# Two of four tiles turned by VectorE and moved in SBUF, in a two-layer kernel on one TensorE

## The chip, the cores and the metric

The kernel runs on one core of one Trainium2 chip. The metric is the device time of one execution in microseconds (us). A core has TensorE (PE in the profile; its weight loads are PEld), VectorE (DVE), ScalarE (ACT), GpSimd (POOL) and SyncE (SP), which issues most of the DMAs. SBUF is the working memory; TensorE writes to PSUM, which has eight banks of 128 x 512 fp32 here.

## The reference

Two transformer layers with a layer norm behind each part, on x of 2 x 512 x 512. Only what the change stands between is shown: the linear attention of layer 0, and behind its norm the quantized feed-forward part.

```python
# layer 0, linear attention (one query head in four is used)
q_sel = (elu(x @ Wq.T + bq) + 1)[:, :, ::G, :]
num = einsum('bshd,hde->bshe', q_sel, M)
den = einsum('bshd,hd->bsh', q_sel, z)[..., None] + EPS
x = layernorm(x + repeat(num / den, G, axis=2).reshape(b, s, H * D) @ Wo.T)
# layer 0, quantized feed-forward; weights are -s, 0 or s
xf = x / 128.0
inter = silu(xf @ w_gate.T) * (xf @ w_up.T)
inter_q = trunc(clip(inter * 128, -128, 127))
x = layernorm(x + trunc(clip(inter_q @ w_down.T * 128, -128, 127)))
# layer 1: softmax attention with one head, then a SwiGLU part, each with a layer norm
```

## The kernel before

x is held as eight tiles of 128 rows x 512, four for each of the two sequences (`xs[b][t]`; `order` lists them as tiles 0 to 7, `NT` is 4). Layer 0's attention first computes the queries, then folds the memory M with the output weights into `mw`.

The stage around the change is the loop over `order` (L677). For each tile, `read` (L550) makes eight products of 128x128 by 128x512 (L561), one per head, each into a PSUM bank of its own; an fp32 product shows as two instructions. The last column of each product is the denominator: ScalarE copies it out (L565), VectorE takes the reciprocal of four at a time (L569). Of the eight heads three are scaled by ScalarE (L574) and added by GpSimd (L578, L590), five are added to x by VectorE (L583). The norm of the tile before (`norm_a0`, L660: statistics on VectorE, the root on GpSimd, the shift at L668 on VectorE and the application at L669 on ScalarE) is put between.

Behind the loop stands the quantized layer, `up` (L733): for each of eleven chunks of the inner width and each sequence, two times eight products in fp32r (L741) with the transposed rows as the moving operand. fp32r keeps fewer bits than fp32, so the rows go in as a high part (a copy rounded to fp32r) and a low part (the rest): `split` (L262) makes both, four column blocks each.

The two sequences get their transposed rows in different ways:

- The first sequence: within tiles 5, 6 and 7 (`halfway`, and behind the tile), TensorE transposes one column block of all four tiles (L275, four transposes into one bank), ScalarE copies it to the high part (L280) and VectorE subtracts for the low part (L281). The high parts lie in one tile of the pool `xtp` (two slots), the low parts in two of the pool `wop` (four slots).
- The second sequence: VectorE turns each tile in squares of 32 x 32 (`turn_squares`, L675), and `move_squares` (L286) moves the squares to their places with 16 SBUF-to-SBUF DMAs over SP, GpSimd and ScalarE (L296). `split(1, xt1)` then copies and subtracts from SBUF.

The first sequence's rows are needed when the loop ends; the second's when six chunks of the first are done (`LEAD`). The down weights' loads wait on SP behind the move.

What sets the order: GpSimd's instructions are issued as written. For the other engines a list scheduler orders them at build time, by the order of the program among those that its cost model holds for ready, so an instruction written later can be issued earlier on its engine. `tc.issue_after(ins)` ties what is written under it to be issued behind `ins`, but only instructions of the same engine as `ins`. On the chip every engine goes through its list in order, and a waiting instruction holds all behind it.

Of the kernel before, what the change touches and what calls it, by code (L numbers as in the profile page):

```python
# [19 lines left out]
P = 128  # L20
# [19 lines left out]
def kernel(  # L40
# [221 lines left out]
    def split(b, xt=None):  # L262


        hi = xtp.tile([P, NK, S], F32, tag="xt", name=f"xh_{b}").bitcast(F32R)
        los = [pair_tile(f"xl_{b}_{i}").bitcast(F32R) for i in range(2)]
        his = [hi[:, k, :] for k in range(NK)]
        los = [los[k // 2][:, k % 2, :] for k in range(NK)]

        def block(k):  # L270
            h, l = his[k], los[k]
            if xt is None:
                rows = psum(f"pt_f0{b}_{k}")
                for t in range(NT):
                    nc.tensor.transpose(rows[:, ts(t, P)], xs[b][t][:, ts(k, P)], ident)  # L275
            else:
                rows = xt[:, :, k, :]
                h, l = (u.rearrange("p (t q) -> p t q", t=NT) for u in (h, l))
            return (
                nc.scalar.copy(h, rows),  # L280
                nc.vector.tensor_sub(l, rows, h.bitcast(F32)),  # L281
            )
# [3 lines left out]
    def move_squares(squares, xt, three=True):  # L286
# [4 lines left out]
        for i in range(P // SQ):  # L291
            for j in range(P // SQ):
                eng = nc.gpsimd if i == j else nc.sync
                if i == (j + 2) % 4:
                    eng = nc.gpsimd if not three else nc.scalar if i else nc.sync
# [8 lines left out]
    def pair_tile(name):  # L304
        return wop.tile([P, 2, HID], F32, tag="wo", name=name)
# [75 lines left out]
    with tc.tile_pool(name="a0w", bufs=1) as a0w, tc.tile_pool(name="a0", bufs=2) as a0:  # L381
# [168 lines left out]
        def read(b, t, halfway, between):  # L550
# [3 lines left out]
            for h0 in range(0, NH, 4):  # L554
                if h0:
                    halfway()
# [114 lines left out]
        x2 = []  # L671

        def turn_squares(i):
# [3 lines left out]
        for i, (b, t) in enumerate(order):  # L677
            steps = read(
                b, t, lambda: block(2 * (i - NT) - 3) if i > NT + 1 else None,
                lambda steps: norm_a0(i - 1, steps) if i else None,  # L680
            )
# [6 lines left out]
            if i == 5:  # L688
                parts, block = split(0)
                x2.append(parts)  # L690
                squares = xtp.tile([P, NT, HID], F32, tag="xt", name="squares")
            if i in (5, 6):
                block(2 * (i - NT) - 2)
            if i > NT:
                turn_squares(i - 1)
        norm_a0(len(order) - 1, steps)
        turn_squares(len(order) - 1)
# [858 lines left out]
```

## Time and profile before

| | us |
|---|---|
| median of three runs (lowest, highest) | 457.17 (457.02, 457.43) |
| the profiled execution | 458.13 |
| its span, first to last instruction | 456.4 |
| TensorE busy | 448.6 |
| VectorE busy | 309.8 |
| ScalarE busy | 259.6 |
| GpSimd busy | 113.7 |

The granted TensorE clock was 0.996 of full speed over the span. In the profile a line such as `106.95 0.44 PE pt_f L275 x4` of the chain in order of time is a start, a length, the engine, the tile written, the line of the program and a count. In the groups of instructions the numbers behind the first bar are the busy time in us and the mean of one in ns; behind the second bar stands the engine's idle time before them, and who ended it. In the timeline the bracket gives the idle time before an instruction and who ended it. Matmul records in the profile overlap, since they are pipelined; their starts tell the pace.

### The profile page before, as it was taken

The numbers are of one execution on the slowest core, as the hardware profiler recorded it, in microseconds if no ns is written. First come the engines' busy times: TensorE is split into PE (matmuls) and PEld (weight loads), VectorE is DVE, ScalarE is ACT, GpSimd is POOL, SyncE is SP. The second block draws the span as 40 slices with busy tenths as digits, with TensorE's granted clock in tenths as the row PEclk, the third lists the DMA queues.
The fourth block names the chain that finished last, engine by engine and source line by source line (L and its number), as shares of the span: only waits on it lengthen the run. The fifth ranks groups of instructions, "written<-read, shape, count | busy, mean of one in ns | idle before, by whom it ended". The sixth has DMA issues, their size and how long they took to land.

```text
span 456.4 us, 5785 instructions
## 1 busy us (share of the span) xinstructions
PE 448.6 (98%) x1913; PEld 337.0 (74%) x1913; DVE 309.8 (68%) x617; ACT 259.6 (57%) x492; POOL 113.7 (25%) x160
## 2 busy tenths in 40 slices
PE   8999999999999999999999999999999999999995
PEld 8887753344588888888766578888888888888884
DVE  3976658777867788856978799545534547777524
ACT  4887986466657974557746645454545446433311
POOL 0200304575640059200372336100000000011211
PEclk9999999999999999999999999999999999999998
DMA  8999981000027201121495601300000000000001
GB/s 278 376 281 314 180 294 46 0 3 0 2 44 198 103 3 48 47 93 37 152 371 87 101 0 31 63 0 1 0 0 1 0 2 0 1 15 33 37 34 69
DMA packets 33172, 38.18 MB, mean 84 GB/s; under 512 B 20656, under 2 KB 21552, under 8 KB 33136
## 3 DMA queue, kind: packets, MB, share of 16 engines
q1 hardware_dynamic: 27440, 30.65, 20.3%
q0 software_dynamic: 2240, 6.29, 7.5%
q10 hardware_dynamic: 3456, 0.75, 0.8%
q8 instruction: 22, 0.36, 0.3%
q14 instruction: 14, 0.11, 0.1%
HBM read 32.45 MB, written 2.10 MB: 76 GB/s over the span
## 4 chain that ended last, share of the span: by engine, by line
PE 92%; DMA 2%; ACT 2%; DVE 1%; issue 1%; SPq 0%; POOL 0%; POOLq 0%
PE pu L1248 23%; PE pd L1248 12%; PE po L561 10%; PE pq L504 9%; PE pg_f L741 9%; PE pu_f L741 9%; PE pd_f L800 4%; PE pqk L1061 3%; PE pu L1293 2%; PE pv L1078 2%; PE pot L1123 2%; PE psc L1017 2%; PE po L1140 2%; DMA gu<-in_gu 1%; DMA wq<-in_wq 1%; PE pmw L545 1%
## 5 line engine op out<-in xcount | busy, mean ns | idle before, releaser
L561 PE MATMUL po<-mw,q 128*128 128x512 f32 x128 | 57.3, 598 | 0.7 <-ACT y L574 0.5
L1248 PE MATMUL pu<-r,ugu 128*128 128x512 f32 x200 | 48.6, 389 | 0.0
L146 POOL TENSOR_TENSOR rstd_f<-mv_f,ln_eps 128x1 f32<-128x1 f32 x15 | 6.1, 409 | 168.7 <-DVE mv_f L1416 128.0
L339 ACT ACTIVATE pu<-pu 128x512 f32<-128x512 f32 x42 | 24.1, 580 | 41.2 <-PE pu L1248 37.4
L561 PEld LDWEIGHTS po<-mw,q 128*128 128x128 f32 x128 | 22.9, 189 | 31.4 <-issue 18.5
L1248 PEld LDWEIGHTS pu<-r,ugu 128*128 128x128 f32 x200 | 37.5, 188 | 7.8
L170 ACT ACTIVATE ta_f<-y_f,below_half 128x512 int8<-128x512 f32 (+1 forms) x22 | 15.9, 721 | 27.4 <-DVE y_f L158 27.1
L583 DVE SCALAR_TENSOR_TENSOR x<-po,den,x 128x511 f32<-128x511 f32 x40 | 29.8, 745 | 1.8
L578 POOL TENSOR_TENSOR y<-y,y 128x511 f32<-128x511 f32 x16 | 21.1, 1319 | 24.9 <-DVE x L583 20.8
L1248 PE MATMUL pu<-r,it_early 128*128 128x512 f32 x104 | 24.9, 389 | 0.0
L767 DVE SCALAR_TENSOR_TENSOR it_f<-tb_f,ta_f 128x512 fp32r<-128x512 int16 (+1 forms) x22 | 15.2, 690 | 13.8 <-ACT tb_f L171 13.8
L741 PE MATMUL pg_f<-xh,tu 128*128 128x512 f32 x88 | 24.4, 399 | 0.0
L1307 DVE TENSOR_TENSOR it_f<-ev,pu 128x512 f32<-128x512 f32 x20 | 13.6, 683 | 15.5 <-PE pu L1248 14.9
L1136 ACT ACTIVATE x<-x,off_f,rstd_f 128x512 f32<-128x512 f32 x7 | 5.7, 816 | 32.0 <-POOL off_f L1135 32.0
L741 PE MATMUL pg_f<-xl,tu 128*128 128x512 f32 x88 | 23.6, 390 | 0.0
L741 PE MATMUL pu_f<-xh,tu 128*128 128x512 f32 x88 | 23.5, 389 | 0.0
L741 PE MATMUL pu_f<-xl,tu 128*128 128x512 f32 x88 | 23.5, 389 | 0.0
L1248 PE MATMUL pd<-ugu,r 128*128 128x512 f32 (+1 forms) x79 | 22.5, 362 | 0.0
L1248 PEld LDWEIGHTS pu<-r,it_early 128*128 128x128 f32 x104 | 19.5, 188 | 4.0
L351 POOL TENSOR_SCALAR td<-wd,inv_down 128x512 fp32r<-128x512 f32 x11 | 20.1, 1846 | 1.6 <-DVE inv_down L206 1.6
L800 PE MATMUL pd_f<-td,it_f 128*128 128x512 f32 x88 | 20.3, 389 | 0.0
L565 ACT ACTIVATE den<-po,den_eps 128x1 f32<-128x1 f32 x64 | 13.6, 271 | 11.1 <-PE po L561 11.0
(382 smaller groups left out, 1089.6 us busy)
## 6 DMA issues: line engine op xcount, KB each, us to landing
gu<-in_gu SPq DMA_DIRECT2D x20, 512.0 KB, 7.4
wd<-in_wd SPq DMA_DIRECT2D x20, 256.0 KB, 4.7
wo<-in_wo SPq DMA_DIRECT2D x8, 512.0 KB, 9.7
wo<-in_wo POOLq DMA_DIRECT2D x8, 512.0 KB, 9.1
wq<-in_wq SPq DMA_DIRECT2D x8, 256.0 KB, 4.9
x<-in_x SPq DMA_DIRECT2D x7, 256.0 KB, 5.1
out<-x SPq DMA_DIRECT2D x7, 256.0 KB, 2.0
x<-in_bo POOLq DMA_DIRECT2D x4, 256.0 KB, 6.1
```

Of the source, the lines that this page charges most:

```text
L170: nc.scalar.activation(a[:n], y, AF.Relu, bias=below_half[:n])
L339: return nc.scalar.activation(p, p, AF.Copy, scale=BIG + 1.0)
L351: eng.tensor_scalar(out, w, factor, None, ALU.mult)
L504: done = nc.tensor.matmul(p, w, x, start=(start and i == 0), stop=(i == len(todo) - 1), skip_group_check=not start,)
L561: nc.tensor.matmul(po, qs[b][h0 + j][:, ts(t, P)], mw[:, h0 + j, :], start=True, stop=True,)
L578: nc.gpsimd.tensor_add(ys[0][:, :LAST], ys[0][:, :LAST], y[:, :LAST])
L583: steps.append(nc.vector.scalar_tensor_tensor(x[:, :LAST], four[j][:, :LAST], d, x[:, :LAST], ALU.mult, ALU.add))
L741: nc.tensor.matmul(pp[a], t[:, a, i % NK, :], x2[b][i], start=(i == 0), stop=(i == 2 * NK - 1),)
L767: nc.vector.scalar_tensor_tensor(it[:n], tb[:n], 128.0, ta[:n], ALU.min, ALU.subtract)
L800: nc.tensor.matmul(pd, inter[b][c][:, ts(t, P)], td[c].bitcast(F32R), start=(c == 0), stop=(c == last),)
L1061: nc.tensor.matmul(p, wqkv[:, k, ts(j, D)], xt[:, k, :], start=(k == 0), stop=(k == NK - 1),)
L1248: done = nc.tensor.matmul(p, w, x, start=(start and i == 0), stop=(i == n - 1), skip_group_check=not start,)
```

## The change

Of the first sequence, tiles 0 and 1 are now turned in squares by VectorE (in the iterations 1 and 2) and moved by 16 DMAs, all issued by SP, with half the bytes each; tiles 2 and 3 are transposed by TensorE tile by tile, four column blocks of one tile into one bank, in iterations 4 and 5. The copies and subtractions go by tile in place of by column block: two halves of 128 x 256 for each tile, from PSUM for tiles 2 and 3 and from the moved squares for tiles 0 and 1 (iterations 5 and 6). The subtractions (and whatever else is VectorE's) of the latter are tied behind the first L583 of their tile. `read` loses its `halfway`. The high and low parts of the first sequence now lie in four tiles of `wop`, those of the second in the two slots of `xtp`. For the other moves nothing is changed.

```diff
+    def split_squares(b, xt):
+        hi, lo = (
+            xtp.tile([P, NK, S], F32R, tag="xt", name=f"x{part}_{b}") for part in "hl"
+        )
+        his, los = units(hi), units(lo)
         def block(k):
-            h, l = his[k], los[k]
-            if xt is None:
-                rows = psum(f"pt_f0{b}_{k}")
-                for t in range(NT):
-                    nc.tensor.transpose(rows[:, ts(t, P)], xs[b][t][:, ts(k, P)], ident)
-            else:
-                rows = xt[:, :, k, :]
-                h, l = (u.rearrange("p (t q) -> p t q", t=NT) for u in (h, l))
+            h, l = (u[k].rearrange("p (t q) -> p t q", t=NT) for u in (his, los))
+            rows = xt[:, :, k, :]
             return (
                 nc.scalar.copy(h, rows),
                 nc.vector.tensor_sub(l, rows, h.bitcast(F32)),
...
+    def split_tiles(b):
+        pairs = [pair_tile(f"x_{b}_{i}", F32R) for i in range(NK)]
+        def part(t, rows):
+            done = []
+            for i in range(2):
+                h, l = (pairs[j + i][:, :, ts(t, P)] for j in (0, 2))
+                src = rows[:, 2 * i : 2 * i + 2]
+                done += [nc.scalar.copy(h, src), nc.vector.tensor_sub(l, src, h.bitcast(F32))]
+            return done
+        def turned(t):
+            rows = psum(f"pt_f0{b}_{t}")
+            for k in range(NK):
+                nc.tensor.transpose(rows[:, ts(k, P)], xs[b][t][:, ts(k, P)], ident)
+            return rows.rearrange("p (k q) -> p k q", k=NK)
+        return [u for p in pairs for u in units(p)], part, turned
...
-    def move_squares(squares, xt, three=True):
+    def move_squares(squares, xt, queues=3):
...
-                eng = nc.gpsimd if i == j else nc.sync
+                eng = nc.gpsimd if i == j and queues > 1 else nc.sync
-                if i == (j + 2) % 4:
-                    eng = nc.gpsimd if not three else nc.scalar if i else nc.sync
+                if i == (j + 2) % 4 and queues > 1:
+                    eng = nc.gpsimd if queues == 2 else nc.scalar if i else nc.sync
...
+        TURNED = NT // 2
         for i, (b, t) in enumerate(order):
-            steps = read(
-                b, t, lambda: block(2 * (i - NT) - 3) if i > NT + 1 else None,
-                lambda steps: norm_a0(i - 1, steps) if i else None,
-            )
+            steps = read(b, t, lambda steps: norm_a0(i - 1, steps) if i else None)
...
-            if i == 5:
-                parts, block = split(0)
+            if i == 1:
+                squares0 = xtp.tile([P, NT, HID], F32, tag="xt", name="squares_0")
+                xt0 = xtp.tile([P, NT, NK, P], F32, tag="xt", name="xt_f00")
+            if 1 <= i <= TURNED:
+                turn_squares(i - 1, squares0)
+            if i == TURNED:
+                move_squares(squares0[:, :TURNED], xt0[:, :TURNED], queues=1)
+            if i == NT:
+                parts, part, turned = split_tiles(0)
                 x2.append(parts)
+                part(TURNED, turned(TURNED))
+            elif i == NT + 1:
                 squares = xtp.tile([P, NT, HID], F32, tag="xt", name="squares")
-            if i in (5, 6):
-                block(2 * (i - NT) - 2)
+                part(NT - 1, turned(NT - 1))
+            if NT + 1 <= i <= NT + TURNED:
+                with tc.issue_after(steps[0].ins):
+                    part(i - NT - 1, xt0[:, i - NT - 1])
             if i > NT:
-                turn_squares(i - 1)
+                turn_squares(i - 1, squares)
...
-        parts, block = split(1, xt1)
+        parts, block = split_squares(1, xt1)
```

More of the change, by code (lines that the diff above doesn't have):

```diff
@@ L260, in down_weights @@
         return wds
[L262 to L268, printed above, removed]
-        def block(k):
-            h, l = his[k], los[k]
-            if xt is None:
-                rows = psum(f"pt_f0{b}_{k}")
-                for t in range(NT):
-                    nc.tensor.transpose(rows[:, ts(t, P)], xs[b][t][:, ts(k, P)], ident)
-            else:
-                rows = xt[:, :, k, :]
-                h, l = (u.rearrange("p (t q) -> p t q", t=NT) for u in (h, l))
+    def split_squares(b, xt):
[3 more added lines that the diff above has]
+        his, los = units(hi), units(lo)
+        def block(k):
+            h, l = (u[k].rearrange("p (t q) -> p t q", t=NT) for u in (his, los))
+            rows = xt[:, :, k, :]
             return (
@@ L302, with pair_tile @@
     wop = ctx.enter_context(tc.tile_pool(name="wop", bufs=4))
-    def pair_tile(name):
-        return wop.tile([P, 2, HID], F32, tag="wo", name=name)
+    def pair_tile(name, dtype=F32):
+        return wop.tile([P, 2, HID], dtype, tag="wo", name=name)
     def spare_tile(name, dtype=F32):
@@ L548, in fold, with read @@
             nc.scalar.activation(mw[:, h, :LAST], p[:, :LAST], AF.Identity, bias=c)
-        def read(b, t, halfway, between):
+        def read(b, t, between):
             x = xs[b][t]
@@ L554, in read @@
             for h0 in range(0, NH, 4):
-                if h0:
-                    halfway()
                 four = []
@@ L671, with turn_squares @@
         x2 = []
-        def turn_squares(i):
+        TURNED = NT // 2
+        def turn_squares(i, squares):
             b, t = order[i]
@@ L687 @@
                 flag_up, eff_up = verdict(tot_up, sc_up, "up")
-            if i == 5:
-                parts, block = split(0)
+            if i == 1:
[7 more added lines that the diff above has]
+                parts, part, turned = split_tiles(0)
                 x2.append(parts)
+                part(TURNED, turned(TURNED))
+            elif i == NT + 1:
                 squares = xtp.tile([P, NT, HID], F32, tag="xt", name="squares")
-            if i in (5, 6):
-                block(2 * (i - NT) - 2)
+                part(NT - 1, turned(NT - 1))
+            if NT + 1 <= i <= NT + TURNED:
+                with tc.issue_after(steps[0].ins):
+                    part(i - NT - 1, xt0[:, i - NT - 1])
             if i > NT:
-                turn_squares(i - 1)
+                turn_squares(i - 1, squares)
         norm_a0(len(order) - 1, steps)
-        turn_squares(len(order) - 1)
+        turn_squares(len(order) - 1, squares)
     fp = ctx.enter_context(tc.tile_pool(name="fp", bufs=2))
@@ L1225 @@
     xt_r1 = fp.tile([P, NT, NK, P], F32, tag="it10", name="xt_f11", bufs=1)
-    move_squares(squares, xt_r1, three=False)
+    move_squares(squares, xt_r1, queues=2)
     def rows_from_squares(k):
```

## The prediction

> **What bounds the kernel now.** I read the page first: the engines' shares and the chain that ended last. TensorE is busy nearly all the time, and 92% of the chain is TensorE.
>
> ```profile
> span 456.4 us, 5785 instructions
> ...
> PE 448.6 (98%) x1913; PEld 337.0 (74%) x1913; DVE 309.8 (68%) x617; ACT 259.6 (57%) x492; POOL 113.7 (25%) x160
> ```
>
> Next the chain in order of time, in the stage that the diff touches: the reading of the memory (L561), with four groups of four transposes (L275) between its products. Right behind it stands the first product of the quantized layer (L741).
>
> ```profile
> 99.98 6.97 PE po L561 x16
> 106.95 0.44 PE pt_f L275 x4
> 107.39 3.44 PE po L561 x8
> 110.82 0.52 PE pt_f L275 x4
> 111.35 3.65 PE po L561 x8
> 114.99 0.44 PE pt_f L275 x4
> 115.43 3.44 PE po L561 x8
> 118.86 0.44 PE pt_f L275 x4
> 119.30 3.44 PE po L561 x8
> 122.74 1.84 PE pg_f L741 x8
> ```
>
> So the sixteen transposes of the first sequence lie on the path, 0.44+0.52+0.44+0.44 = 1.84 us of it. From 122.74 to 445.5 us the chain is TensorE without a stall worth naming, so what TensorE gains here should reach the end, unless another engine hands over late.
>
> Which other engine is close? The eight products of tile 2 take 6.87 us of TensorE, undisturbed (first products start at 78.44 and 85.31). In the chain, 6.97 against 6.87, 0.52 against 0.44 and 3.65 against 3.44 are waits of 0.10, 0.08 and 0.21 us, 0.39 together, for a PSUM bank: there are eight, a tile has eight products, and VectorE (L583) or ScalarE (L574) frees each. These two form a loop, and the timeline of VectorE shows it:
>
> ```profile
> 84.15 0.17 DVE L569 RECIPROCAL den<-den 128x4 f32<-128x4 f32 x1
> 84.41 0.75 DVE L583 SCALAR_TENSOR_TENSOR x<-po,den,x 128x511 f32<-128x511 f32 x1
> 87.45 0.18 DVE L569 RECIPROCAL den<-den 128x4 f32<-128x4 f32 x1 [2.29 <-ACT den L565]
> ...
> 91.48 0.17 DVE L569 RECIPROCAL den<-den 128x4 f32<-128x4 f32 x1
> ```
>
> From the first reciprocal of a tile to that of the next it is 91.48-84.15 = 7.33 us, above TensorE's 6.87. VectorE idles only in one place, 2.29 us behind L583, while ScalarE does a norm, three scalings and four denominators. Work in that hole is free; work elsewhere in the loop is not.
>
> **What goes.** Half of the transposes of L275, eight of sixteen: two undisturbed groups of four, 2 x 0.44 = 0.88 us of TensorE. Also gone are four copies and four subtractions of 128x512 (rows below): 4 x 0.60 = 2.4 us of ScalarE, 4 x 0.67 = 2.7 us of VectorE. Their banks, held for the time from transposes to subtraction (106.95 to 111.24 for the first), fall from four to two.
>
> ```profile
> L675 DVE STREAM_TRANSPOSE squares<-x 128x512 f32<-128x512 f32 x4 | 2.8, 704 | 0.8 <-ACT x L669 0.8
> ...
> L281 DVE TENSOR_TENSOR xl<-pt_f,xh 128x512 fp32r<-128x512 f32 x4 | 2.7, 666 | 0.5 <-ACT xh L280 0.5
> ...
> L280 ACT CAST xh<-pt_f 128x512 fp32r<-128x512 f32 x4 | 2.4, 599 | 0.2 <-PE pt_f L275 0.2
> ```
>
> **What comes.**
> Two VectorE transposes of 128x512: 2 x 0.71 = 1.41 us. Each waits for its tile's norm on ScalarE (84.27 to 85.09 for tile 0; 91.60 to 92.41 for tile 1) and is ready just when the hole behind L583 opens; the two that exist in this stage stand there too (114.07, 121.63). I cost them at nothing; elsewhere in the loop they would be 0.71 each, and tiles 0 and 1 are far enough ahead of TensorE's need to win nothing.
> Eight copies and eight subtractions of 128x256. The nearest rows of that size, median in the middle, are two copies of the first rows:
>
> ```profile
> L458 ACT COPY xt_raw<-pt_a x4: 353/370/373, 5.7 to 10.1; 128x256 f32<-128x256 f32 x4
> L459 DVE COPY xt_raw<-pt_a x4: 411/424/425, 6.1 to 10.8; 128x256 f32<-128x256 f32 x4
> ```
>
> That makes 8 x 0.37 = 2.96 and 8 x 0.42 = 3.39 us, 0.56 and 0.73 more than what goes. The four subtractions fed from the squares are ordered behind the first L583 of their tile, so they open in the hole (2 x 0.42 beside 0.71 of a transpose, under 2.29): nothing; each waits for its copy on ScalarE, and behind it on VectorE stands the tile's second reciprocal, which needs 2.29 us anyway. The four fed from PSUM come ahead of the next tile's reciprocal: in the loop, up to 4 x 0.42 = 1.7 us. Before, of the four subtractions, those at 110.58 and 118.17 stood in the loop (0.57 and 0.58 from start to start) and one copy (114.66) held back the denominators by 0.46: 1.6 us. I take the loop as unchanged over tiles 4 to 7: the two sums lie within a tenth. The ends are 1.6 us sooner (all four fall in the hole) and 1.3 us later (four copies also fall ahead of the denominators, at 0.3 each: 0.37 less the overlap that 0.58 against 0.46 shows at 114.66).
> Sixteen DMAs on SP, 32 KB each. SP has nothing between 63.6 and 132.63 us, so only they themselves wait there, for the second transpose; behind them is the other move and the loads of the down weights, tens of us later. No queue of POOL or ScalarE is touched. An issue takes 0.64 us (median of L296 on SP) with about 0.03 between: 16 x 0.67 = 10.7 us. From 93.2 (norm at 92.41, transpose 0.71) they are all issued at 103.9 and, at 2.0 to 2.3 us from issue to landing for that form, landed at about 105.5. The one long issue of the other move, 2.08 us, would make it 107.
> Two transpose groups that move to tiles 4 and 5: tile 2 is normed at 99.90, when TensorE ends tile 4 (99.84): a wait between nothing and 0.1 us, with tile 5's products behind it; I take 0.05. Buffers: the second sequence's low parts move into the slot of the squares, whose readers must land anyway before the copies start: nothing. The first sequence's parts take all four slots of the pair tiles, whose readers (L540) end at 61 us: nothing.
>
> **The handover that takes a part back.** The second sequence's parts come from the loop's end: last norm 130.91, transpose 131.76, SP's move from 132.63 (nine issues, 7.76 us), and then four copies (L280) from 142.18 and four subtractions (L281). The last subtraction (start 144.72, 0.69) ends at 145.41 and its product starts at 145.95: 0.54 us of slack. The copies started 0.34 behind the landing (141.84), because ScalarE was still at L171, which follows TensorE. So TensorE can come about 0.8 us sooner before it waits here, if VectorE's loop ends when it does now.
>
> **Sum.** TensorE -0.88; the bank waits of 0.39 us I keep; the handover gives back 0.88-0.80 = 0.08 with the loop unchanged. That is -0.80; 0.05 goes to the wait at tile 2: -0.75. Against the profiled execution's own 458.13 us (span 456.4 and 1.73 around it) that makes 457.4. That execution lay 0.96 over the median of the runs, 457.17, so I predict 456.4 us. A measurement tells about 0.2%, 0.91 us, from no change, so this gain lies just inside.
>
> A rule speaks against the change: the Trainium skill, "VectorE: DVE Perf Modes", section "Rules for kernel authors", says to turn 128x128 on TensorE wherever the result may go to PSUM, and leaves VectorE the 32x32 case. By it the move would win nothing, and the time would stay at 457.2. The same page ("The three transpose paths") gives 390 ns to a 128x128 bf16 transpose on TensorE; eight would be an estimated 3.1 us, and the time 454.1. This trace has 0.44 us for four, in a stage where TensorE is the one that all wait for, and the sum above goes by that.
>
> **The rivals.**
> A. Full gain and fewer waits. Two banks instead of four are held by transposed rows, the last ones long before the stage ends, and tile 7 has no subtractions any more (118.17 and 120.40 go). Then the 0.39 of bank waits go as well, and the loop ends sooner, so the handover takes nothing: -0.88-0.39 = -1.27, 455.9 us. Against it: tiles 4 and 5 get more work than before.
> B. The loop becomes the bound. With the late end above (1.3 us) the second sequence's parts come 1.3 later, less 0.8 of slack: +0.5, 457.7. Between, at 0.8 later, it is zero. For it: 7.33 against 6.87. Against: the hole of 2.29.
> C. Slower: ScalarE stands before the squares. The copies from the squares are tied to no place on ScalarE (the order of L583 binds VectorE's instructions only). ScalarE waits 0.60 us for TensorE ahead of each denominator between 101.84 and 104.42; a copy queued there waits for the landing at 105.5 to 107, and behind it stand the denominators, the norm and the scalings of that tile, then VectorE's reciprocal, then TensorE's banks. The reciprocal of 105.15 would come 1.5 to 3 us later; less 0.8 of slack that is +0.7 to +2.2, middle +1.5, 458.7. It turns the sign once ScalarE stands for over 0.8 us, the slack. For it: 105.5 is past the tile's denominators. Against: a copy put behind the scalings (107.7) waits for nothing.
> D. That the change does nothing: excluded, as the transposes lie on the chain; all of it hidden behind the handover is a case of B.
>
> **How the numbers follow.** The forecast 0.50 (own range -1.2 to -0.3: 456.0 to 456.9), A 0.16, B 0.15, C 0.19. Faster by over 0.91 us: all of A and 0.38 of the forecast, 0.35. Slower by over 0.91: 0.85 of C and 0.1 of B, 0.18. Same: 0.47. The range goes from 455.6 (A with some waits of tiles 3 and 4 gone) to 458.6 (half of C): left out are half of C, 0.09, and little of A.
>
> **What would show it.** Right: eight transposes of rows instead of sixteen, two groups of 0.44 in the chain; the first L741 product at about 121.9; two VectorE transposes in the hole near 85 and 92.5; sixteen SP issues from 93 to 104; the first copy from the squares with no idle time before it. Wrong: ScalarE idle for a DMA ahead of a copy (C), reciprocals over 7.4 us apart in tiles 4 to 6 (B), or TensorE waiting at the first product of the second sequence near 143.6.

## The result: a quarter of a per cent slower

The changed kernel takes 457.88 us (median; 457.08 to 459.54), the kernel before, run between, 457.23: the ratio is 1.0023, 95% interval 1.0013 to 1.0032, so it is slower by 0.6 to 1.5 us. The forecast of 456.4 had the sign wrong; the time lies within the range that went with it.

Two stretches of the profile carry the comparison, measured from marks that nothing earlier can shift. The **stage** goes from the first product of tile 2 to the first product of the quantized layer; the **stretch** goes on from tile 2 to the first down product, so it takes in the handover to the second sequence as well. Before, the stage was 43.73 us and the stretch 121.54; now they are 43.42 and 123.01. A second profile of each kernel gave 43.74 and 121.54, and 43.40 and 123.02. So the change gains 0.31 us in the stage and loses 1.78 behind it, 1.47 in all in the profiles. The medians are only 0.65 us apart, and 1.47 lies at the upper end of the interval of the times. (When tile 2 starts differs from execution to execution, 76.5 to 78.5 us over all these kernels; the medians hold that too.)

The page's first lines answer to those shown of before: eight matmuls and eight weight loads fewer on TensorE, as written, and the same busy time to a tenth.

```profile
span 456.0 us, 5807 instructions
...
PE 448.6 (98%) x1905; PEld 335.5 (74%) x1905; DVE 312.6 (69%) x623; ACT 259.8 (57%) x496; POOL 114.9 (25%) x160
```

TensorE's timeline of the changed kernel (start, length, line, count). Two groups of transposes (L296) are left where there were four, 0.49 and 0.44 us from their start to the next product's; but not all of what is gone is gained: tile 7, which has no group any more, takes 6.94 us from its first product to the first of the quantized layer (113.12 to 120.07), where it took 6.91 with one (115.27 to 122.17). And behind the last products with the rows of the first sequence (`x`) TensorE waits for the second's (`xh`): the product due at 142.17 starts at 142.88, and those behind it wait too, 1.86 us in all.

```profile
98.19 0.66 PE L296 MATMUL pt_f<-ident,x 128*128 128x128 f32 x4
98.68 7.10 PE L574 MATMUL po<-mw,q 128*128 128x512 f32 x16
105.61 0.60 PE L296 MATMUL pt_f<-ident,x 128*128 128x128 f32 x4
106.05 14.48 PE L574 MATMUL po<-mw,q 128*128 128x512 f32 x32
120.07 2.31 PE L763 MATMUL pg_f<-x,tu 128*128 128x512 f32 x8
...
140.36 1.98 PE L763 MATMUL pu_f<-x,tu 128*128 128x512 f32 x8
142.88 2.06 PE L763 MATMUL pg_f<-xh,tu 128*128 128x512 f32 x4 [0.55 <-ACT xh L274]
```

Before, it went straight on to the second sequence (from 144.36; the high parts of both are called `xh` there), four products every 0.91 us:

```profile
143.45 1.07 PE L741 MATMUL pu_f<-xl,tu 128*128 128x512 f32 x4
144.36 1.07 PE L741 MATMUL pg_f<-xh,tu 128*128 128x512 f32 x4
145.27 1.07 PE L741 MATMUL pg_f<-xl,tu 128*128 128x512 f32 x4
```

The chain that ended last shows who is late. Before, it was TensorE from the reading stage on. Now it leaves TensorE and runs through VectorE's loop, the last turned square and the issues of the second move on ScalarE's queue (ACTq) to ScalarE's copies:

```profile
113.67 1.72 DVE x L290 x2
...
127.44 0.61 DVE squares L689
...
131.18 0.45 ACTq L311
131.66 2.32 ACTq L311
134.00 0.67 ACTq L311
...
142.23 0.61 ACT xh L274
142.88 0.49 PE pg_f L763
```

Two pieces in it are longer than any of their kind before: a pair of subtractions of 1.72 us, and one DMA issue of 2.32. Each turned out to be a cause of its own.

### The profile page after: what moved, and what is told of

Its sections match the earlier page's. It is cut to its first block, busy times and chain, and to the rows that moved or that the text cites. A ratio compares the mean times of both kernels' runs of the same rounds, so it can differ in the third digit from the quotient of the medians.

```text
span 456.0 us, 5807 instructions
## 1 busy us (share of the span) xinstructions
PE 448.6 (98%) x1905; PEld 335.5 (74%) x1905; DVE 312.6 (69%) x623; ACT 259.8 (57%) x496; POOL 114.9 (25%) x160
## 4 chain that ended last, share of the span: by engine, by line
PE 84%; DVE 7%; ACT 3%; issue 3%; POOL 1%; ACTq 1%; POOLq 0%; DVEq 0%
PE pu L1270 23%; PE pd L1270 12%; PE pq L519 9%; PE pg_f L763 7%; PE pu_f L763 6%; PE po L574 6%; PE pd_f L822 4%; DVE x L596 4%; PE pqk L1083 3%; PE pu L1315 2%; PE pv L1100 2%; PE pot L1145 2%; PE psc L1039 2%; PE pmw L560 2%; PE po L1162 2%
## 5 line engine op out<-in xcount | busy, mean ns | idle before, releaser
L170 ACT ACTIVATE ta_f<-y_f,below_half 128x512 int8<-128x512 f32 (+1 forms) x22 | 15.9, 721 | 28.7 <-DVE y_f L158 24.4
L763 PE MATMUL pg_f<-x,tu 128*128 128x512 f32 x88 | 22.1, 393 | 0.0
L763 PE MATMUL pu_f<-x,tu 128*128 128x512 f32 x88 | 21.7, 389 | 0.0
L763 PEld LDWEIGHTS pg_f<-x,tu 128*128 128x128 f32 x88 | 16.5, 188 | 3.9 <-DVE x L596 0.4
L763 PEld LDWEIGHTS pu_f<-x,tu 128*128 128x128 f32 x88 | 16.5, 188 | 3.4
```

The lines of the kernel that those rows point to most:

```text
L170: nc.scalar.activation(a[:n], y, AF.Relu, bias=below_half[:n])
L763: nc.tensor.matmul(pp[a], t[:, a, i % NK, :], x2[b][i], start=(i == 0), stop=(i == 2 * NK - 1),)
```

## The experiments

In the diffs the changed kernel is the one with the minus, except where another is named. "Landed" and "copies" are counted from the end of the last turned square; the copies are ScalarE's first of the second sequence (L274). "Load" is the first load of TensorE's code near the second move, from the same square; negative is ahead of it. "Wait" is TensorE's at the handover. Of after_early, which moves in two parts, landing and copies are those of the second part.

| kernel | load | ScalarE's issues | landed | copies | wait | stage | stretch | ratio to before (95%) |
|---|---|---|---|---|---|---|---|---|
| before | 1.8 | 2.12 | 9.37 | 9.71 | 0 | 43.73 | 121.54 | |
| changed | 1.1 | 3.78 | 10.86 | 11.37 | 1.86 | 43.42 | 123.01 | 1.0023 (1.0013 to 1.0032) |
| after_pe | -2.3 | 2.10 | 8.78 | 9.68 | 0 | 44.25 | 122.06 | 1.0004 (0.9994 to 1.0014) |
| after_early | 2.0 | 2.37 | 11.38 | 11.64 | 1.76 | 43.43 | 122.88 | 1.0037 (1.0024 to 1.0050) |
| after_pad32 | -1.9 | 2.36 | 8.41 | 9.94 | 0.45 | 43.41 | 121.58 | 0.9996 (0.9984 to 1.0009) |
| after_pad128 | 5.9 | 2.35 | 9.30 | 9.95 | 0.45 | 43.41 | 121.57 | 1.0005 (0.9992 to 1.0019) |
| after_pad224 | 2.1 | 2.35 | 9.50 | 9.95 | 0.02 | 43.43 | 121.67 | 1.0000 (0.9986 to 1.0013) |
| after_nomove | 1.5 | 3.09 | 8.84 | 10.67 | 0.78 | 42.94 | 121.54 | 0.9986 (0.9970 to 1.0002) |
| after_2q | 1.0 | none | 11.34 | 11.82 | 3.81 | 43.45 | 124.98 | 1.0021 (1.0000 to 1.0043) |
| after_sp12 | 1.7 | none | 12.33 | 12.51 | 2.95 | 43.42 | 124.08 | 1.0044 (1.0030 to 1.0057) |
| after_half | 2.2 | 2.35 | 9.44 | 9.94 | 0 | 44.80 | 122.61 | 1.0020 (1.0002 to 1.0038) |
| after_half_pad32 | -2.0 | 2.35 | 8.46 | 9.94 | 0 | 44.80 | 122.60 | 1.0015 (1.0000 to 1.0030) |
| after_half_2q_pad32 | -1.9 | none | 8.99 | 9.52 | 0 | 44.82 | 122.62 | 1.0022 (1.0006 to 1.0037) |
| after_swap | 1.5 | 2.90 | 9.11 | 10.48 | 0.57 | 42.98 | 121.38 | 1.0019 (1.0006 to 1.0032) |
| after_swap_pad32 | -1.4 | 2.36 | 8.49 | 9.94 | 0.02 | 42.98 | 120.81 | 0.9999 (0.9988 to 1.0011) |
| both_again (the same kernel) | -2.0 | 2.36 | 8.47 | 9.95 | 0.03 | 42.97 | 120.83 | 0.9984 (0.9971 to 0.9997) |
| before_pad32 | -2.0 | 2.11 | 9.77 | 9.94 | 0 | 43.74 | 121.54 | 0.9999 (0.9985 to 1.0012) |

### Is it the first move at all?

My first theory had no cause yet, only a place: what TensorE gains earlier is lost at the handover. The pair itself was profiled again beside the first two kernels.

> The kernel before, unchanged, for a second profile. Handover theory (the second sequence's squares land late and TensorE waits at its first product): no wait of TensorE there, the parts end before they are needed, about 0.5 us of slack, 9 to 10 us from the last turned square to the last landing. Chance theory (the long move in the profile of the changed kernel is luck): 9 to 11 us here, and now and then a wait of up to 1 us.

> The changed kernel, unchanged, for a second profile. Handover theory: TensorE waits again at the first product of the second sequence, 0.5 to 2 us, whatever its lead at the start of the read stage. Loop theory (the read stage itself gains nothing, as its waits for banks grow): the stage from tile 2 to the first product of the quantized layer takes 43.4 us again instead of 42.8 (43.7 less 0.88). Chance theory: the move takes 9 to 11 us here as before, and the wait at the handover is gone.

The first kernel leaves VectorE's squares of tiles 0 and 1 and their move out and transposes these tiles on TensorE as well; the parts are made tile by tile as in the changed kernel.

```diff
-            if 1 <= i <= TURNED:
-                turn_squares(i - 1, squares0)
-            if i == TURNED:
-                move_squares(squares0[:, :TURNED], xt0[:, :TURNED], queues=1)
...
-                    part(i - NT - 1, xt0[:, i - NT - 1])
+                    part(i - NT - 1, turned(i - NT - 1))
```

> The changed kernel with one part undone: tiles 0 and 1 are transposed by TensorE too, tile by tile, in tiles 5 and 6, with no squares and no first move. Handover theory: the read stage grows by up to 0.88 us, but TensorE would have waited at the handover anyway, so the total stays within 0.4 us of the changed kernel. If TensorE's time in the read stage reached the end, 0.5 to 0.9 us slower than the changed kernel. If the first move on SP or its copies are what costs, 0.5 or more faster than the changed kernel.

The second relieves the handover: tiles 4 and 5 of the second sequence are moved early, by SyncE alone, into a place that a later weight had (its load goes behind), and the final move carries tiles 6 and 7 only.

```diff
+            if i == NT + 2:
+                move_squares(squares[:, :2], early1, queues=1)
...
-    moved = move_squares(squares, xt1)
+    moved = move_squares(squares[:, 2:], xt1)
```

> The changed kernel with the squares of tiles 4 and 5 moved as soon as tile 5 is turned, by SP alone, and only those of tiles 6 and 7 at the end, over three queues with half the bytes each. Handover theory: the wait at the first product of the second sequence goes, so 1.0 to 1.9 us less than the changed kernel, 0.1 to 0.9 less than before. Loop theory: the time of the changed kernel within 0.3 us.

The second profiles repeated everything: 1.88 us of wait, and none before. Without the squares the wait was gone, and the move landed after 8.78 us instead of 10.86, although its code is the same; the stage grew by 0.83 us over the changed kernel's, and the stretch still fell by 0.95. With the early move the wait stayed at 1.76: SyncE was still issuing sixteen early DMAs of 0.6 to 0.7 us when the last square was turned, and the others came behind them. So the place was right, the remedy was none, and the question became why an untouched move takes two microseconds more.

### Sixteen DMAs on the queue, or loads of code?

The record of DMA packets has an answer that I had overlooked. Beside data there are queues of kind "instruction". This is the DMA view of the time from the last square to the landing, first of the changed kernel, then of the one before (packets, MB, share; of the latter without its last 0.3 us, in which another packet starts, at 141.53, when all of the move's own are through):

```profile
q8 instruction: 2, 0.03, 1.6%
q14 instruction: 1, 0.01, 0.3%
```

```profile
q8 instruction: 1, 0.02, 1.1%
```

A packet of q8 is 16 KB and takes 0.9 to 2.1 us, where a packet of the move takes 0.01. It is TensorE's code: late in the kernel, in the changed one, the packets come at 315.88, 344.72 and 373.85 us, and between two of them TensorE executes 128 or 129 weight loads (PEld) and 129 or 130 matmuls, 257 and 259 together with those that the edges cut. That is one instruction for every 64 bytes of a packet. The view of busy time by stretches (in brackets the instructions):

```profile
315.88:344.72 28.84, 28.84 (x129) 23.89 (x128) 12.09 (x19) 14.91 (x26) 0.00 (x0) 1.00 0.00 1
344.72:373.85 29.13, 29.13 (x130) 24.13 (x129) 16.44 (x26) 13.94 (x26) 0.00 (x0) 1.00 0.00 0
```

In the second move of the changed kernel such packets start at 131.91 (1.56 us) and 139.18 (1.25 us), and one of 8 KB on q14 at 137.89. (A packet of q14 near this move, from 4 us ahead of the last square on, is there in every kernel whose SyncE issues a first move and in none of the others; so the change seems to have brought this one itself. That it is SyncE's code is inferred from this.) ScalarE's issue of 2.32 us runs from 131.66 to 133.98 and one of SyncE's from 132.31 to 133.98: the first begins 0.25 us ahead of the first packet's start, the other 0.40 behind it, and both end at the same instant, 0.5 us behind its end. Before, the packet came at 134.32, when ScalarE had begun its last issue; one SyncE issue, 134.26 to 136.34, took the 2.08 us that the prediction had noticed and not explained.

Moved code tells the two theories apart. Each chunk of the quantized layer has a branch that is never taken here. Matmuls put there never run, but all code behind them lies further on.

```diff
             with way.Else():
+                for _ in range(8 if (b, c) == (0, 0) else 0):
+                    nc.tensor.matmul(
+                        pp[0][:n], gus[c][:, 0, 0, :], x2[b][0].bitcast(F32),
+                        start=True, stop=True,
+                    )
                 for a in range(2):
```

> Eight matmuls that never run are put into the branch of the first up chunk that is not taken (about 32 instructions), so all code of TensorE behind it lies 2 KB further on; nothing else changes. In the four profiles so far the second move takes 8.78 us where no load of code falls between the last square and the last landing, 8.94 and 9.37 where one of 0.96 or 1.52 us does, and 10.86 and 11.27 where three of 3.28 and 3.17 us together do. Theory 'code loads': the two loads of TensorE's code (11.8 and 19.1 us behind the first up product) come at other places, the move takes 8.8 us plus about 0.7 of the loads that fall in it, and TensorE's wait at the handover, 1.86 us now, changes by as much; with one load fewer the time goes down by 0.6 to 1 us. Rival 'SyncE's history': the sixteen earlier DMAs on SyncE's queue slow the second move; it stays at 10.9 to 11.3 us and the wait at 1.8 to 1.9, the time at that of the changed kernel.

> As the kernel with 32 instructions of padding, with 32 matmuls that never run (about 128 instructions, half a block of code). 'Code loads': TensorE's loads move by about half of their spacing, so that at most one of them falls in the second move: the move at 9.3 to 10 us, the wait 0.3 to 1.0, the time 0.8 to 1.5 us below the changed kernel's. 'SyncE's history': move 10.9 to 11.3 us, wait 1.8 to 1.9, no gain.

> As before with 56 matmuls that never run (about 224 instructions, a block but for 32). 'Code loads': as if the code lay 32 instructions nearer; if the load at 19.1 us behind the first up product comes a chunk later (22.7), it lies behind the move, the move takes 9.3 to 9.9 us and the time is 1.0 to 1.8 us below the changed kernel's; if it stays, nothing is gained. 'SyncE's history': move 10.9 to 11.3 us, wait 1.8 to 1.9, no gain.

The fourth leaves the first move out, and with it SyncE's sixteen DMAs; a tile that nothing else uses keeps the slot of the moved squares.

```diff
+                free = xtp.tile([P, NT, NK, P], F32, tag="xt", name="free")
+                nc.gpsimd.memset(free[:, :1, :1, :1], 0.0)
...
-                xt0 = xtp.tile([P, NT, NK, P], F32, tag="xt", name="xt_f00")
...
-                move_squares(squares0[:, :TURNED], xt0[:, :TURNED], queues=1)
+                xt0 = squares0.rearrange("p t (k i) -> p t k i", k=NK)
```

> The changed kernel without its first move: the parts of tiles 0 and 1 are read from the tile of turned squares itself, so these two tiles' rows are not what the reference computes; all else is as in the changed kernel, and SyncE's sixteen earlier DMAs are not there. 'SyncE's history': the second move is back at 8.8 to 9.4 us, the wait at 0 to 0.3, the time 1.5 to 1.9 us below the changed kernel's. 'Code loads': TensorE's two loads stay where they are, and only the load of SyncE's own code (0.4 us) moves: the move takes 10.3 to 11 us, the wait 1.3 to 1.9, the time at most 0.5 us below the changed kernel's.

With all three paddings the loss of the changed kernel was gone: the move landed after 8.41, 9.30 and 9.50 us with all sixteen DMAs of the first move still there, and the stretch fell by 1.34 to 1.44 us. SyncE's history is out as the cause. With 32 the first load comes 1.9 us ahead of the last square; with 128 at 5.9 us; with 224 it comes 2.1 us behind the square, when ScalarE's issues are nearly over. With 32 and 128 a wait of 0.45 us is left. The 0.02 with 224 is no gain: there TensorE lost about 0.5 us at its second chunk (groups of eight products start at 123.62, 125.83 and 127.75, 2.21 and 1.92 apart instead of 1.81), for a cause that these runs don't show. ScalarE's timeline with 32:

```profile
130.93 2.36 ACTq L311 DMA_DIRECT2D xt_f<-squares  x3
133.34 0.72 ACT L170 ACTIVATE ta_f<-y_f,below_half 128x512 int8<-128x512 f32 x1 [2.61 <-DVE y_f L158]
...
140.84 1.65 ACT L274 CAST xh<-xt_f 128x512 fp32r<-128x512 f32 x3
```

and in the changed kernel:

```profile
130.89 3.78 ACTq L311 DMA_DIRECT2D xt_f<-squares  x3
134.72 0.72 ACT L170 ACTIVATE ta_f<-y_f,below_half 128x512 int8<-128x512 f32 x1 [4.03 <-issue]
...
142.23 1.12 ACT L274 CAST xh<-xt_f 128x512 fp32r<-128x512 f32 x2
```

In both the first `ta` (L170) starts 0.05 us behind ScalarE's last issue, and the copies 7.50 us behind that `ta`: 133.34 to 140.84, 134.72 to 142.23. In the kernel before it is 134.68 to 142.18. What lies between is ScalarE's own list, with one wait of 1.32 us for VectorE's `y`, which itself follows ScalarE's work. With 32 the rows had landed 1.54 us before the copies began; the copies did not wait for them.

Without the first move neither theory's numbers held: 8.84 us for the move fits the history, a wait of 0.78 does not, and I had been wrong that TensorE's loads would stay where they were, because the loop ended 0.8 us sooner, and so the squares moved against the loads. That shorter loop was the next question: the stage fell to 42.94 us, and VectorE's work was the same.

### ScalarE's issues or the landing?

Here the second move is put on SyncE and GpSimd alone (eight each), and in another kernel ScalarE's three issues are given to SyncE (twelve, GpSimd four).

```diff
-    moved = move_squares(squares, xt1)
+    moved = move_squares(squares, xt1, queues=2)
```

> The changed kernel with the second move on SyncE (8) and GpSimd (8), none on ScalarE. In every profile so far ScalarE's first copy of the moved rows starts 7.50 us behind its first ta (four ta and tb, two silu and a wait for y lie between), and ta starts when ScalarE's three issues of the move end: 134.63 in the kernel before (last square at 132.47), 134.67 in the changed kernel (last square at 130.86, one issue of 2.32 us), 133.3 in the kernel padded by 32. Theory 'ScalarE is held by its issues, and these by a load of TensorE's code': with no issue on ScalarE ta starts at the y it needs, about 1.5 us behind the last square, and the copies at about 9.0 us behind it or 0.3 us behind the landing, whichever is later; with the loads of code still where they were (11.8 and 19.1 us behind the first up product) and a move of 9.5 to 11 us the copies start 0.3 to 1.6 us sooner than now, the wait at the handover goes from 1.86 to 0.3 to 1.6, and the time is lower by as much. Rival 'only the landing counts': the move stays at 10.9 to 11.3 us or grows, since GpSimd issues twice as many, and the wait stays at 1.8 or more.

```diff
-                    eng = nc.gpsimd if queues == 2 else nc.scalar if i else nc.sync
+                    eng = nc.gpsimd if queues == 2 else nc.scalar if i and three else nc.sync
...
-    moved = move_squares(squares, xt1)
+    moved = move_squares(squares, xt1, three=False)
```

> The changed kernel with ScalarE's three issues of the second move given to SyncE (SyncE 12, GpSimd 4 as before). 'ScalarE is held by its issues': its first ta starts 1.5 to 1.7 us behind the last square for 3.86 now, and the copies are then bound by the landing alone (twelve issues of 0.65 on one queue, and the loads of code: 10.5 to 12 us behind the last square), 0.3 to 0.5 us behind it, not right behind the last tb; the wait at the handover 1.0 to 2.4 us. Rival: ta stays at 3.5 us or more behind the last square, since something else holds ScalarE.

ScalarE in the kernel without its issues (two queues):

```profile
132.59 0.72 ACT L170 ACTIVATE ta_f<-y_f,below_half 128x512 int8<-128x512 f32 x1 [0.51 <-DVE y_f L158]
...
144.07 1.14 ACT L274 CAST xh<-xt_f 128x512 fp32r<-128x512 f32 x2 [2.33 <-DMA wd<-in_wd]
```

Free of its issues ScalarE starts `ta` 0.34 us behind the last square in both kernels (2.2 before, 3.9 changed), sooner than the 1.5 that I had expected: so it was the issues that held it. Then the copies wait for the landing (2.33 and 2.38 us; the name in the bracket of this one is that of a neighbouring DMA, but the copies start 0.48 us behind the move's own landing), and the landing is later with fewer queues, 11.34 and 12.33 us. For the wait, the landing theory was right about two queues. Together, with the move on three queues: the copies start 7.50 us behind the first `ta`, which follows ScalarE's issues, or 0.2 to 0.5 us behind the landing, whichever is later. In the changed kernel the loads of code push both: 142.23 by the one, about 142.0 by the other. In its second profile the landing was the later: the copies came 0.18 us behind it and 7.79 behind `ta`. Freeing one alone could have gained little, and both tries at it made the landing later.

### Why does the stage gain 0.31 us and not 0.75?

Without the first move VectorE had the same instructions, but two pairs of subtractions at other places in its list, and the stage was 0.48 us shorter. First try: its order forced on the changed kernel, with the parts of tiles 0 and 1 issued between the halves of tiles 5 and 6 and the second reciprocal tied behind them; once alone, once with the padding, once also with the move on two queues.

```diff
             for h0 in range(0, NH, 4):
+                before = halfway() if h0 else ()
...
-                nc.vector.reciprocal(den, den)
+                with ExitStack() as tied:
+                    for step in before:
+                        tied.enter_context(tc.issue_after(step.ins))
+                    nc.vector.reciprocal(den, den)
```

> The changed kernel with the low and high parts of tiles 0 and 1 issued between the two halves of tiles 5 and 6, in front of the second reciprocal, so that VectorE does tile 0's two subtractions in its idle time of 2.1 us in tile 5 and tile 1's in tile 6, one of them on each side of the turned square. Theory 'order': in the changed kernel two of these subtractions and one of 1.48 us stand in front of the two reciprocals of tile 6 and end the loop 0.8 us later than the same kernel without the first move, whose order this is; so the stage from tile 2 to the first up product takes 42.9 to 43.0 us for 43.4, and the last square comes 0.7 to 0.8 us sooner. The handover is as bad as now (loads of code at the same distances from the first up product): total 0 to 0.8 us below the changed kernel. Rival 'the first move itself delays the loop' (by its landing, or by its traffic): the stage stays at 43.4.

> Both of these together: the order of the parts, and eight matmuls that never run, which move TensorE's loads of code. 'Order' and 'code loads' add up: the stage at 42.9 to 43.0 us, the move at 8.4 to 9.3 us, the wait at the handover 0.2 to 0.8; from tile 2 to the first down product 121.0 to 121.2 us (before 121.54, changed 123.01), the time 0.3 to 0.6 us below the kernel before. If the handover takes all back, 121.5 and no gain.

> All three: the order of the parts, the padding by 32, and the second move without ScalarE. The copies start 9.0 to 9.6 us behind the last square, TensorE waits 0 to 0.3 us at the handover, tile 2 to the first down product 120.7 to 121.0 us, the time 0.5 to 0.9 us below the kernel before. If the landing on two queues is what is late: the move over 10 us, the wait 0.5 or more, no better than the kernel with two of the three.

All three missed: the stage became 44.8 us. VectorE, then TensorE, of after_half:

```profile
108.57 2.14 DVE L290 TENSOR_TENSOR x<-xt_f,x 128x256 fp32r<-128x256 f32 x2 [1.96 <-ACT x L290]
110.63 0.17 DVE L586 RECIPROCAL den<-den 128x4 f32<-128x4 f32 x1
```

```profile
111.70 1.12 PE L575 MATMUL po<-mw,q 128*128 128x512 f32 x2 [1.16 <-DVE x L600]
```

The subtractions stood where they should, but ScalarE's copies, which they need, still stood behind the three scalings; VectorE waited 1.96 us for them, the reciprocal came late, TensorE waited 1.16 for a bank. The order had been copied for one engine of two. The wait at the handover is 0 in all three, since TensorE comes later; the loss in the stage seems to reach the total, ratios of 1.0015 to 1.0022 for 1.06 to 1.08 us (1.0023), though the intervals begin at 1.0000 to 1.0006.

The 2.14 us in that line hold one subtraction of 1.49 us (109.22 to 110.71); it starts 0.13 us behind an addition of GpSimd (109.09 to 110.42) and ends 0.29 behind its end. The changed kernel has one as well, in the pair of 1.79. VectorE, then GpSimd, in the changed kernel:

```profile
112.96 0.70 DVE L689 STREAM_TRANSPOSE squares<-x 128x512 f32<-128x512 f32 x1
113.59 1.79 DVE L290 TENSOR_TENSOR x<-xt_f,x 128x256 fp32r<-128x256 f32 x2
115.31 0.16 DVE L582 RECIPROCAL den<-den 128x4 f32<-128x4 f32 x1
```

```profile
111.39 1.84 POOL L603 TENSOR_TENSOR x<-x,y 128x511 f32<-128x511 f32 x1 [1.14 <-DVE x L596]
113.67 2.84 POOL L591 TENSOR_TENSOR y<-y,y 128x511 f32<-128x511 f32 x2 [0.43 <-ACT y L587]
```

The second subtraction of the pair starts at 113.89, 0.22 us behind the first of the two additions of the last line (113.67 to 115.10), and ends 0.28 behind its end. The other seven subtractions of the first sequence, the four fed from PSUM among them, take 0.38 to 0.42 us. The cure to try is one exchange: tile 4's turned square behind the subtractions, so that both come before the addition.

```diff
-                    part(i - NT - 1, xt0[:, i - NT - 1])
-            if i > NT:
+                    done = part(i - NT - 1, xt0[:, i - NT - 1])
+            if i == NT + 2:
+                with tc.issue_after(done[1].ins), tc.issue_after(done[3].ins):
+                    turn_squares(i - 2, squares)
+            if i > NT + 1:
                 turn_squares(i - 1, squares)
```

> The changed kernel with one pair of VectorE's instructions exchanged: tile 4's turned square is issued behind tile 1's two subtractions instead of in front of them. Theory 'GpSimd': the subtraction of 1.49 us (all others 0.31 to 0.42) starts 0.2 us after an addition of GpSimd and ends 0.3 us after that one does, so it waits for it; its operands both lie in SBUF, while those that run freely beside GpSimd read a PSUM bank. Issued 0.6 us sooner both end before the addition begins: 0.3 to 0.7 each, the second reciprocal of tile 6 at 37.8 to 38.0 us behind tile 2's first product for 38.65, the last square 0.6 to 0.8 us sooner, the stage from tile 2 to the first up product 42.9 to 43.0 us for 43.4. Rival 'the tile' (whatever else is slow in reading the moved tile): the subtraction stays at 1.4 to 1.5 us wherever it stands, the stage at 43.4. The handover stays bad, so the total is 0 to 0.8 us below the changed kernel's.

> The exchange, and the eight matmuls that never run. 'GpSimd' and 'code loads' together: the stage at 42.9 to 43.0 us, the wait at the handover 0.1 to 0.8, tile 2 to the first down product 120.8 to 121.3 us (before 121.54, changed 123.01, changed with padding 121.58), the time 0.2 to 0.7 us below the kernel before. If the handover takes all of it back: 121.5 and the time of the kernel before.

The control, padding in the kernel before, and the last kernel once more:

> Control: the kernel before with the same eight matmuls that never run. 'Code loads': its loads move too (the one at 12.1 us behind the first up product to 8 to 9 us or not at all), but its handover has no wait to lose, so tile 2 to the first down product stays at 121.5 us and the time within 0.15% of the kernel before. Rival 'padding is good in itself': 1 us or more faster, as in the changed kernel.

> The kernel with the exchange and the padding once more, for a narrower answer on the total: from tile 2's first product to the first down product it was 0.73 us shorter than the kernel before, which is 0.9984 of the time, but its ratio came out at 0.9999 with an interval from 0.9988 to 1.0011. If the 0.73 us reach the end: 120.8 us in that stretch again and a ratio of 0.998 to 0.999. If something outside the stretch takes them back: 120.8 again and a ratio of 0.9995 or more.

VectorE, then GpSimd, with the exchange: the pair takes 0.89 us, and its second subtraction (114.31, 0.41 us) has started when the addition starts (114.54).

```profile
113.83 0.89 DVE L290 TENSOR_TENSOR x<-xt_f,x 128x256 fp32r<-128x256 f32 x2
114.65 0.70 DVE L689 STREAM_TRANSPOSE squares<-x 128x512 f32<-128x512 f32 x1
115.37 0.18 DVE L582 RECIPROCAL den<-den 128x4 f32<-128x4 f32 x1
```

```profile
114.54 2.66 POOL L591 TENSOR_TENSOR y<-y,y 128x511 f32<-128x511 f32 x2 [0.43 <-ACT y L587]
```

The second reciprocal of tile 6 comes at 37.84 us behind tile 2's start instead of 38.66, the last square 0.79 us sooner, and the stage takes 42.98 us: 0.75 below the kernel before. So it was the place in the order, not the moved tile. The row agrees with a rule of the Trainium skill, "SBUF — State Buffer", section "Who interferes with whom": a VectorE instruction with two SBUF inputs and a GpSimd instruction that reads SBUF exclude each other, and the later one waits for the whole of the other. The other way round shows too: GpSimd's addition at 111.39, just behind a subtraction at 111.35, takes 1.84 us; in the kernel without the first move the same addition, with no subtraction beside its start, takes 1.27:

```profile
112.13 1.27 POOL L603 TENSOR_TENSOR x<-x,y 128x511 f32<-128x511 f32 x1 [1.14 <-DVE x L596]
```

The exchange alone has a ratio of 1.0019, as bad as the changed kernel, though its one profile shows a stretch of 121.38 with a wait of 0.57; there the load overlapped ScalarE's last issue (1.20 us long) instead of its second. Whether its other executions fared worse isn't known. With the padding as well, the stretch is 120.81 and 120.83, 0.73 and 0.71 below before, and TensorE goes from the first sequence to the second without a wait (both_again):

```profile
140.42 1.98 PE L766 MATMUL pu_f<-x,tu 128*128 128x512 f32 x8
142.23 1.07 PE L766 MATMUL pg_f<-xh,tu 128*128 128x512 f32 x4
```

Its ratio was 0.9999 the first time and 0.9984 the second, 456.14 against 456.73 us; 0.72 us is 0.9984. The second interval, 0.9971 to 0.9997, holds that and leaves 1 out, the first (0.9988 to 1.0011) does not hold it: the gain is real in the profile and likely, not certain, in the time. The control settles the padding: the load moved by one chunk in the kernel before too (1.8 us behind the square to 2.0 ahead), and nothing changed, 121.54 and 0.9999. It is no gain in itself; it takes away a loss.

## Why the prediction was wrong, by its own steps

- **The 0.88 us of TensorE.** Two groups are gone from the timeline, and with the loop undisturbed the stage is 0.75 shorter (after_swap), for 0.83 in the sum (0.88 less 0.05 at tile 2). In the changed kernel it was 0.31. The step that failed is "I take the loop as unchanged over tiles 4 to 7": the subtraction fed from the squares was priced at 0.42 us by a row that reads PSUM. That held for three of the four; the fourth started beside a GpSimd addition, which the prediction did not look at, and took 1.49. It delayed tile 6's second reciprocal by 0.8 and the last square by as much, against -0.61 without it; so the last square came 0.18 us later than before, counted from tile 2. The total of the loop was thus within the range given (1.6 sooner to 1.3 later), by a cause not in it.
- **Where the subtractions open.** "In the hole" was wrong: the list scheduler put tile 0's behind the idle time of tile 5, in front of tile 6's first reciprocal (111.35, 111.68). The hole of 2.1 us (104.86 to 106.99) stayed empty; the copies that they need started only at 107.07 on ScalarE.
- **The two squares** cost nothing, as said: 83.34 and 90.67, in the hole. **The sixteen DMAs** were issued from 91.41 to 101.95, 0.61 us each but the first, and had landed at 103.26, for 103.9 and 105.5 forecast; as tile 2 began 1.79 us sooner in this execution, that is 0.2 sooner and 0.5 sooner than forecast, counted from there.
- **Rival A** fell: with the loop undisturbed 0.75 of the 0.88 arrive, so the waits for banks did not go. What is missing stands at tile 2's transposes: from the start of tile 4's last product to that of tile 5's first it is 1.18 us in after_swap (98.36 to 99.54) and was 0.57 (99.27 to 99.84), so this group costs 0.61 us where it stands instead of 0.44, and the term of 0.05 was 0.17. **Rival C** fell: ScalarE's four copies from the squares (107.07 to 108.14) waited for nothing. **Rival B** came near in its result, the parts arriving too late, not by its cause.
- **The handover gives back 0.08.** This is the step that turned the sign: it gave back 1.78, and TensorE's wait at the second sequence's first product, the last of the prediction's own signs of being wrong, was there. Of the wait of 1.86 us, 0.45 are left with the padding by 32, and 0.02 with the exchange as well: taken in this order, 1.41 came with the loads of code and 0.43 with the late end of the loop. Two parts of the step were wrong. The slack of "about 0.8" was 0.54 + 0.34, and the 0.34 came from reading that ScalarE "was still at L171, which follows TensorE"; the runs show that this list hangs on the end of ScalarE's own three issues, 7.55 us ahead of the copies. And the second move was left unchanged as its code is; but TensorE's code is loaded by DMA, at a place set by TensorE's progress (the first load near the move starts 12.15 us behind the first product of the quantized layer before, 11.84 in the changed kernel), while the squares follow VectorE's. The read stage got 0.3 shorter and TensorE's code sixteen instructions shorter, the loop did not, and the first load came 1.05 us behind the last square instead of 1.85, into ScalarE's second issue (3.78 us for three instead of 2.12), and the second load, with the one on q14, into the tail of the move.
- **The unexplained row.** The prediction used the one long issue of 2.08 us as a bound for the first move, never asking what it was. The loads had been in the page of before, in the list of DMA queues.
- **The rule against the change** (VectorE's transposes) had no part in it: the squares were free.

## What to carry to other kernels

Ask of a gain on the bounding engine what else is tied to that engine's progress: here its code loads, which slide against transfers that another engine starts, and can cost more than was won; code put where it never runs tells in one run whether an unexplained microsecond is such a collision. When VectorE reads two operands from SBUF, look at what GpSimd does at that time: the price of such a subtraction alone was right here, and the one beside an addition took 1.49 us for 0.42. And where a copy starts just behind a landing, follow its engine's list back to what released it before calling that the slack.

## What the runs showed of the hardware

- A load of 16 KB of TensorE's code takes one DMA packet of 0.9 to 2.1 us. On ScalarE and SyncE every issue of the second move that took over 1.3 us, up to 2.32 for 0.6 to 0.7, had such a load within it; not every issue with one was long (ScalarE's third in the kernel before: 0.67), and some of SyncE's took 0.8 to 1.3 us with none. From the last square to the landing the move took 8.4 to 8.9 us with up to 1.4 us of loads in it, 9.1 to 9.8 with 1.2 to 2.4, and 10.9 to 11.3 with 3.2 to 3.3 (moves on three queues with SyncE free). The Trainium skill, "Runtime: NRT & Kernel Launch", section "Instruction fetch mechanics", has the 16 KiB blocks and the DMA queue of the sequencer's own, and calls the cost mostly hidden; in the changed kernel no wait of TensorE itself stands at a load, but ScalarE's and SyncE's issues were held.
- Where the code lies decides it: 8 to 56 matmuls that never run shortened the stretch by 1.3 to 1.4 us in the changed kernel, and 8 of them did nothing to it in the kernel before.
- Which load hits which issue is steady: two profiles of the changed kernel have the first load at 1.05 us behind the last square, and waits of 1.86 and 1.88.
- GpSimd as issuer: with eight of sixteen DMAs on it instead of four, and none on ScalarE, the move with loads in it took 11.34 us; with loads out of the way 8.99, against 8.46 with four.
